# Layer 1's rest blocks: matrices in buffers of their own, names fetched three blocks ahead, the last certain block split around a turn

## The chip, the cores and the metric

The kernel runs on one core of a Trainium2 chip. The core has a matrix engine (TensorE, PE in the profile), a vector engine (DVE), a scalar engine (ACT), GpSimd (POOL) and SyncE (SP), each with a queue of its own that it works through in order, and 16 DMA engines that they all share. The metric is the device time of one execution in microseconds; less is better. Before the change the median of three runs is 1893.99 us.

## The reference, cut to what matters

The model has four layers. Each adds a graph part and a feed-forward part to `x`, of 2708 rows by 256. The change touches the feed-forward part of layer 1 only:

```python
    def _L1_ffn_ref(x, W1, b1, Wg, bg, Wd, bd):
        ...
        H = jax.nn.gelu(xf @ W1 + b1, approximate=False)
        probs = jax.nn.softmax((H @ Wg + bg) / TEMP, axis=-1)
        assign = jnp.argmax(probs, axis=-1)
        out = jnp.zeros_like(xf)
        for e in range(Wd.shape[0]):
            y = H @ Wd[e] + bd[e]
            sel = (assign == e)[:, None]
            out = out + jnp.where(sel, probs[:, e:e + 1] * y, 0.0)
        return out.reshape(orig_shape)
    ...
    x = x + _L1_ffn_ref((_layernorm(x, axis=-1))[None], L1_ffn_W1, L1_ffn_b1, L1_ffn_Wg, L1_ffn_bg, L1_ffn_Wd, L1_ffn_bd)[0]
```

There are 8 experts. A row of `H` has 1024 numbers, an expert matrix `Wd[e]` is 1024 by 256, and each row goes to one expert, the one with the largest gate value.

## The kernel before, in words

**Layer 1 in three groups of row tiles.** The 22 tiles of 128 rows (the last has 20) are worked in the groups `GROUPS1`: 8, 8 and 6 tiles. For each group the graph part streams the adjacency matrix through TensorE (L1312). Then `send1` (L1122) handles the group: it turns the normalised rows (L220), computes the hidden rows with Gelu (`hidden`, L375 and L377), computes the gate, takes the softmax and the largest value, and calls `route` (L385). `route` counts with a few small matmuls (L402 and L404) where in a list sorted by expert each row belongs. Each row's name (its number and gate value, 8 bytes) is then scattered to that place of the list `taken` in main memory (L513). `keep` (L1162) transposes the hidden rows on DVE (L1169) and writes them to `hid` in main memory; in the last group from SP (L1174 and L1177).

**Blocks.** The list is worked in blocks of 128 names of one expert. After the second group 9 blocks (`NA`) are certain to be full, whatever the third group brings; these are known while the third group's graph part still runs. The other 15 (`ALWAYS`), the rest, are laid out by `blocks` (L423) after the third group's route, because their names include that group's. More than these are worked in a branch (`run_rest`) that is taken only if some are left. So 24 blocks run in all, each with these steps in the class `Units` (L638):

- `fetch_names` (L653) gathers a block's names from `taken` with an indirect DMA of POOL (L527). It has to come after the scatters listed in `past`.
- `fetch_rows` (L663) gathers the block's 128 hidden rows, 4 KB each, from `hid` into one of four `hs` buffers with an indirect DMA of POOL (L667). It needs the block's names, and the buffer has to be free of the turn of four blocks before.
- `weights1` (L1070) loads the expert matrix (1152 KB with its bias) from SP (L1077) into one of three `wb` buffers; the load is skipped at run time if that buffer already holds this expert. Blocks are taken in the order of `in_thirds`, so that each buffer sees neighbouring blocks, often of one expert. The expert's number is read from a table in SBUF into a register of SP.
- `turn` (L673) transposes the rows on TensorE (L678, 8 instructions), and ACT copies the result to `hTs` (L679).
- The products (L729, 16 instructions of 128x256 output columns: 8 chunks of the 1024, two passes each), then the bias and the gate value on DVE (L730 and L731), and a scatter of the 128 results to `given` from POOL (L513).

`pieces` (L709) is a generator that yields after each turn and each block's products: the turn of the first block, then for every block the turn of the next and the block's own products. `send1` of the third group calls `next(fill)` to put the first pieces between its own stages. `more` (L689), called in every block, fetches names one block ahead of the rows, rows into free buffers and matrices two blocks ahead. `add` (L698) appends the rest blocks, once `blocks` has laid them out.

**What sets the order.** A scheduler puts each engine's instructions in order by dependencies and its own estimates; `after`, `engine_after` and `in_order` (L147 to L165) add orders by hand. The gate's tiles (weights of the gate, `hT`, `hrow`, the softmax and route tiles, `names`) lie in the pool `gt`, closed at L1350. SBUF that a closed pool leaves can be used by a later pool; each new tile then waits for the last readers of what lay there. When all results have landed in `given`, layer 2 reads them (`mine`, L56) and adds them to `x` (L1441).

The functions that the change touches:

Of the kernel before, what the change touches and what calls it, by code (L numbers as in the profile page):

```python
# [66 lines left out]
def adj_ffn4(ctx: ExitStack, tc: tile.TileContext, a: dict, out: bass.AP):  # L67
# [570 lines left out]
    class Units(Blocks):  # L638
# [3 lines left out]
        def __init__(self, pool, given, weights, hidden):  # L642
            Blocks.__init__(self, pool, given, weights)
            self.hidden, self.named, self.places, self.got = hidden, [], [0, 0], None

            self.names = pool.tile([P, MOST, 2], F32, name="names")
            g.memset(self.names, 1.0)
            self.hs = [pool.tile([P, HC * P], F32, name="hs", tag="hs", bufs=3) for _ in range(3)]
            for h in self.hs:
                g.memset(h, 0.0)  # L650
            self.ik, self.ok, self.outputs = "taken1", "given1", 0
# [11 lines left out]
        def fetch_rows(self):  # L663
            m, n = self.named.pop(0)
            h = self.hs[self.places[1] % len(self.hs)]
            self.places[1] += 1
            i = g.indirect_dma_start(out=h, out_offset=None, in_=self.hidden[:n, :],  # L667
                                 in_offset=bass.IndirectOffsetOnAxis(ap=m[:, 0:1].bitcast(I32), axis=0),
                                 bounds_check=n - 1, oob_is_err=False)
            self.got = i.ins.name  # L670
            self.rows.append((m, h))
# [10 lines left out]
        def begin(self, items):  # L682

            self.names_todo = list(items)
            self.todo = list(items)
            self.rows_todo = len(items)
            self.more(False)

        def more(self, weights=True):  # L689
            while self.names_todo and len(self.named) + len(self.rows) < len(self.hs) + 1:  # L690
                self.fetch_names(self.names_todo.pop(0))
            while self.rows_todo and len(self.rows) < len(self.hs):
                self.fetch_rows()
                self.rows_todo -= 1
            while weights and self.todo and len(self.ahead) < 2:
                self.fetch(self.todo.pop(0))

        def add(self, items):  # L698
            self.names_todo += items
            self.todo += items  # L700
            self.rows_todo += len(items)
            self.more()
# [6 lines left out]
        def pieces(self, pool, during=None):  # L709
# [4 lines left out]
            while self.rows:  # L714
                if len(self.rows) > 1:
                    turned.append(self.turn(pool, self.rows[1][1]))
                    yield
                w2, hT = self.ahead.pop(0), turned.pop(0)
# [8 lines left out]
                q = pools["psum"].tile([P, W], F32, name="yacc", bufs=2)[:, :D]  # L727
                for f in range(HC):
                    te.matmul(q, lhsT=hT[:, f, :], rhs=w2[:, f, :], start=(f == 0), stop=(f == HC - 1))  # L729
                v.tensor_tensor(y, q, w2[:, HC, :], ALU.add)  # L730
# [327 lines left out]
    with ExitStack() as l1:  # L1058
# [5 lines left out]
        wbs, reads = {"held": []}, []  # L1064
# [5 lines left out]
        def weights1(b, e):  # L1070

            held = wbs["held"]
            if len(held) < 3:
                held.append([wbs["pool"].tile([P, 2048 + D], F32, name="wb", bufs=3), None])
# [47 lines left out]
        def send1(tiles, ready=None, fill=None):  # L1122
# [3 lines left out]
            names = gt.tile([P, GM, 2], F32, name="names", bufs=1)[:, :G]  # L1126
# [84 lines left out]
            if ready is not None:  # L1211
                for _ in range(3):
                    next(fill)
            ix = route(gt, (sel,), G, t0 * P, rows(tiles[-1]), known)
            if ready is not None:
                in_order(start, (mybir.EngineType.PE,))
                keep(*was, nc.sync)
            for i, t in enumerate(tiles):
                r = rows(t)
                scatter(taken[1], ix[:r, i, :], names[:r, i, :], N - 1, "taken1")  # L1220

# [128 lines left out]
        gate.close()  # L1350
        past = list(scattered["taken1"])
# [5 lines left out]
        for one in wbs["held"]:  # L1357
# [755 lines left out]
```

## Time and profile before

| what | value |
|---|---|
| three runs | 1893.95, 1893.99, 1900.85 us |
| profiled execution, whole time | 1890.82 us |
| its span, first to last instruction | 1889.1 us |
| mean granted TensorE clock | 0.985 |
| first and last products of L729 start | 944.9 and 1059.4 us |
| L729, matmuls | 384, median 379 ns |
| L678, transposes | 192, median 273 ns (pipelined: eight take 0.87 us in the chain) |
| L1077, matrix loads issued from SP | 24, 1152 KB each where not skipped |
| L667, L527 gathers on POOL | median 1029 and 1002 ns of POOL's time; 4.6 and 4.3 us to landing |

The stretch of the change is thus about 920 to 1072 us of the span: the last gates, the 24 blocks, and the hand-over to layer 2. A line of the timeline reads: start, duration, engine, line, operation, output and inputs, count, and in brackets the idle time of the engine before it and what ended that. A line of the waits reads: who waited, for whom, total us, times, longest. A chain of waits lists, in order of time, what the end of the span hung on.

### The profile page before, as it was taken

Reading aid. Unit: us, or ns where it says so; the run is one execution under the profiler, and the core shown is the slowest. Engines: PE = TensorE matmul, PEld = TensorE weight load, DVE = VectorE, ACT = ScalarE, POOL = GpSimd, SP = SyncE. Lnnn points to the kernel's source line nnn. Section 1 sums busy time; section 2 is a strip of 40 time slices with the busy share of each in tenths; the row PEclk is TensorE's granted clock in tenths of the full one; section 3 lists DMA queues with packets and bytes.
Section 4 is the critical chain, followed back from the end, with each engine's and each line's share of the span. In section 5 each row is a group of like instructions: output and inputs, shape, how many; then the busy total and the mean of one; then the engine's idle time right before and its main releaser. Section 6 shows DMA issues by size and latency. Waiting matters only on the chain.

```text
span 1889.1 us, 25828 instructions
## 1 busy us (share of the span) xinstructions
PE 1816.3 (96%) x9453; PEld 1331.8 (70%) x9453; DVE 1072.4 (57%) x2451; ACT 655.3 (35%) x1472; POOL 393.3 (21%) x466
## 2 busy tenths in 40 slices
PE   8999999999999999999999699998899999999998
PEld 7888788888888888887788588887566633233344
DVE  8687872443343424444532365555345498888877
ACT  8777742222223203112322223223233542132232
POOL 0015354333321002303357400000000100011020
PEclk9999999999998999999999899999899999999999
DMA  8535658887763453644777440000101000012020
GB/s 272 156 100 165 227 193 295 320 313 295 277 265 125 141 152 103 173 119 121 209 235 250 159 65 9 1 1 1 45 1 35 17 1 23 23 26 37 23 37 18
DMA packets 93214, 237.52 MB, mean 126 GB/s; under 512 B 18288, under 2 KB 49048, under 8 KB 85017
## 3 DMA queue, kind: packets, MB, share of 16 engines
q1 hardware_dynamic: 71512, 189.18, 30.9%
q0 software_dynamic: 21568, 46.61, 9.0%
q8 instruction: 78, 1.28, 0.3%
q14 instruction: 56, 0.45, 0.1%
HBM read 218.39 MB, written 30.80 MB: 132 GB/s over the span
## 4 chain that ended last, share of the span: by engine, by line
PE 40%; DMA 4%; DVE 3%; issue 2%; ACT 1%; POOL 1%; POOLq 0%; SPq 0%; ACTq 0%; DVEq 0%
PE num L2014 10%; PE ps_acc L1548 9%; PE den L2022 6%; PE ps_tmp L375 4%; PE ps_acc L1757 3%; PE ps_tmp L267 2%; PE yacc L729 2%; DMA names<-taken,b_ix 1%; DMA hs<-hid,names 1%; DMA L_gnn_a_r<-in_L_gnn_a_r 1%; PE ps_acc L267 1%; DVE e L1985 1%; DMA mine<-given 1%; PE ps_acc L678 1%; PE ps_tmp L220 0%
## 5 line engine op out<-in xcount | busy, mean ns | idle before, releaser
L1985 DVE SCALAR_TENSOR_TENSOR e<-arena,G,mask 128x1024 f32<-128x1024 f32 (+1 forms) x252 | 275.0, 1149 | 34.1 <-PE den L2022 33.2
L2014 PE MATMUL num<-e,wh 128*64 128x512 f32 (+4 forms) x1056 | 214.0, 549 | 0.7 <-ACT L_gnn_W L1368 0.3
L1548 PE MATMUL ps_acc<-hh,e 128*128 128x257 f32 x882 | 199.2, 382 | 1.7 <-ACT o L1491 1.7
L1312 PE MATMUL acc<-sup,adrow 128*128 128x256 f32 x882 | 198.5, 382 | 1.5 <-DMA adrow<-in_adjT 1.5
L943 PE MATMUL acc<-msg,wt 128*128 128x256 f32 x882 | 197.6, 381 | 1.6 <-DVE wt L893 1.2
L1312 PEld LDWEIGHTS acc<-sup,adrow 128*128 128x128 f32 x882 | 165.1, 190 | 29.4 <-issue 5.5
L1548 PEld LDWEIGHTS ps_acc<-hh,e 128*128 128x128 f32 x882 | 163.8, 190 | 29.1 <-ACT o L1491 4.3
L943 PEld LDWEIGHTS acc<-msg,wt 128*128 128x128 f32 x882 | 165.1, 190 | 27.0 <-DVE wt L893 1.8
L591 PE MATMUL ps_acc<-xTs,wa 128*128 128x256 f32 (+1 forms) x768 | 169.3, 373 | 2.6 <-DVE xTs L581 2.6
L593 ACT ACTIVATE hTs<-ps_acc,wa 128x256 f32<-128x256 f32 (+1 forms) x192 | 88.7, 464 | 235.2 <-PE yacc L625 160.8
L625 PE MATMUL yacc<-wb,hTs 128*128 128x256 f32 x736 | 168.4, 380 | 0.0
L591 PEld LDWEIGHTS ps_acc<-xTs,wa 128*128 128x128 f32 x768 | 136.6, 190 | 28.6 <-DVE xTs L581 5.1
L2014 PEld LDWEIGHTS num<-e,wh 128*64 128x64 f32 (+1 forms) x1056 | 70.1, 136 | 122.7 <-issue 104.9
L625 PEld LDWEIGHTS yacc<-wb,hTs 128*128 128x128 f32 x736 | 137.2, 190 | 17.8 <-DVE ys L627 0.5
L1540 DVE SCALAR_TENSOR_TENSOR e<-Rb,G,mask 128x640 f32<-128x640 f32 (+2 forms) x110 | 85.0, 774 | 91.1 <-PE ps_acc L1548 90.4
L2022 PE MATMUL den<-e,wh 128*32 128x512 f32 (+4 forms) x1056 | 112.3, 546 | 0.0
L1277 DVE TENSOR_SCALAR mask<-adrow 128x1024 uint8<-128x1024 f32 (+1 forms) x66 | 41.7, 632 | 120.3 <-DMA adrow<-in_adjT 120.2
L221 ACT COPY xT<-ps_tmp 128x256 f32<-128x256 f32 x76 | 26.8, 366 | 198.9 <-PE ps_tmp L220 198.4
L729 PE MATMUL yacc<-wb,hTs 128*128 128x256 f32 x384 | 88.3, 384 | 0.8 <-DMA wb<-in_L_ffn_Wdp 0.8
L893 DVE SCALAR_TENSOR_TENSOR wt<-adrow,wt 128x640 f32<-128x640 f32 (+3 forms) x67 | 71.1, 1063 | 25.4 <-ACT wt L141 25.1
L2022 PEld LDWEIGHTS den<-e,wh 128*32 128x32 f32 (+1 forms) x1056 | 33.1, 109 | 73.6 <-issue 69.6
L513 POOL DMA_INDIRECT given<-ys,xs x46 | 65.8, 1431 | 81.1 <-DVE ys L628 67.9
(472 smaller groups left out, 2631.0 us busy)
## 6 DMA issues: line engine op xcount, KB each, us to landing
adhalf<-in_adjT SPq DMA_DIRECT2D x42, 677.0 KB
wb<-in_L_ffn_W2p SPq DMA_DIRECT2D x24, 1152.0 KB
wb<-in_L_ffn_Wdp SPq DMA_DIRECT2D x24, 1152.0 KB
wa<-in_L_ffn_W1b SPq DMA_DIRECT2D x24, 1028.0 KB
adrow<-in_adjT SPq DMA_DIRECT2D x42, 512.0 KB
adrow<-in_adjT SPq DMA_DIRECT2D x42, 320.0 KB
adrow<-in_adjT SPq DMA_DIRECT2D x21, 576.0 KB
adrow<-in_adjT SPq DMA_DIRECT2D x21, 448.0 KB
```

The lines of the kernel that those rows point to most:

```text
L375: te.matmul(p[:, :w], lhsT=w1[:, c, f * P : (f + 1) * P], rhs=xnT[:, c, c0 : c0 + w], start=(c == 0), stop=(c == DC - 1))
L591: i = te.matmul(p[:, f % 2, : m * P], lhsT=w1[:, c, f * P : (f + 1) * P], rhs=xT[:, c, : m * P], start=(c == 0), stop=(c == DC - 1))
L593: s.activation(hT[:, f, : m * P], p[:, f % 2, : m * P], AF.Gelu, bias=bias[:, f : f + 1])
L625: te.matmul(q[:, k, :], lhsT=hT[:, f, k * P : (k + 1) * P], rhs=w2[:, f, :], start=(f == 0), stop=(f == HC - 1))
L729: te.matmul(q, lhsT=hT[:, f, :], rhs=w2[:, f, :], start=(f == 0), stop=(f == HC - 1))
L943: te.matmul(p[:q, n - pair[0], :], lhsT=wt[:, k : k + q], rhs=msg[:r, j, :], start=(j == 0 and n == pair[0]), stop=(j == FULL - 1 and n == ...
L1312: te.matmul(p[:q, n - pair[0], :], lhsT=ad[:, k : k + q], rhs=sup[:, jj, :], start=(jj == 0 and n == pair[0]), stop=(jj == FULL - 1 and n ...
L1540: i = v.scalar_tensor_tensor(e[:r, :w], Rb[:r, c0 : c0 + w], G[:r, j, :], mask[:r, j, c0 : c0 + w], op0=ALU.max, op1=ALU.mult)
L1548: te.matmul(p[:, : D + 1], lhsT=e[:, k : k + q], rhs=hh[:, j, :], start=(j == 0), stop=False)
L1985: v.scalar_tensor_tensor(e[:, :w], slow[:, m % 2, k, :w], G[:, j, 2 * pair + k, :], mask[:, j, c0 : c0 + w], op0=ALU.max, op1=ALU.mult)
L2014: te.matmul(num[k * DK : (k + 1) * DK, hf, :q], lhsT=wh[some, j, 2 * pair + k, :DK], rhs=e[some, :q], start=(j == 0), stop=(j == FULL), ti ...
L2022: te.matmul(den[z * Q : (z + 1) * Q, :q], lhsT=wh[some, i, 2 * pair + k, DK : DK + 1] .to_broadcast([some.stop - some.start, Q]), rhs=e[so ...
```

## The change

- The rest blocks get matrix buffers of their own: three `wb` tiles in a new pool `w1r`, opened when the gate's pool `gt` is closed, and a list `rest` of their own in `wbs` and in `Units` (`fetch_rest`). `add` fetches three of them at once; later two are kept ahead. The first load into each of the three is not conditional.
- `names` of `send1` moves from `gt` to the pool `hw` (tile `sent`).
- Names: three blocks are fetched at the start, then one ahead among the certain blocks, and up to three ahead from the ninth row gather on.
- The third group's route is put before the products of block 1 (`range(2)` in place of `range(3)`), and the last pair's transposes on DVE are ordered behind the third DVE instruction of the route.
- The row gather of the eighth block is ordered behind the last scatter into `taken`.
- For the ninth block, the last certain one (`late`), the turn of the next block no longer stands before its products but before the last two of its eight chunks, with TensorE's order fixed.

```diff
@@ -646,6 +646,7 @@
             self.names = pool.tile([P, MOST, 2], F32, name="names")
             g.memset(self.names, 1.0)
             self.hs = [pool.tile([P, HC * P], F32, name="hs", tag="hs", bufs=3) for _ in range(3)]
+            self.past, self.border, self.rest, self.rest_ahead = None, None, [], []
             for h in self.hs:
                 g.memset(h, 0.0)
             self.ik, self.ok, self.outputs = "taken1", "given1", 0
@@ -667,6 +668,8 @@
             i = g.indirect_dma_start(out=h, out_offset=None, in_=self.hidden[:n, :],
                                  in_offset=bass.IndirectOffsetOnAxis(ap=m[:, 0:1].bitcast(I32), axis=0),
                                  bounds_check=n - 1, oob_is_err=False)
+            if self.past is not None and self.places[1] == self.border - 1:
+                after(i, self.past)
             self.got = i.ins.name
             self.rows.append((m, h))
 
@@ -682,23 +685,36 @@
         def begin(self, items):
 
             self.names_todo = list(items)
+            self.border = self.border or len(items)
             self.todo = list(items)
             self.rows_todo = len(items)
+            for _ in self.hs:
+                self.fetch_names(self.names_todo.pop(0))
             self.more(False)
 
         def more(self, weights=True):
-            while self.names_todo and len(self.named) + len(self.rows) < len(self.hs) + 1:
-                self.fetch_names(self.names_todo.pop(0))
             while self.rows_todo and len(self.rows) < len(self.hs):
+                if not self.named:
+                    self.fetch_names(self.names_todo.pop(0))
                 self.fetch_rows()
                 self.rows_todo -= 1
+            while self.names_todo and len(self.named) < (3 if self.places[1] >= self.border else 1):
+                self.fetch_names(self.names_todo.pop(0))
             while weights and self.todo and len(self.ahead) < 2:
                 self.fetch(self.todo.pop(0))
+            if weights:
+                self.fetch_rest(2)
+
+        def fetch_rest(self, most):
+            while self.rest and len(self.rest_ahead) < most:
+                self.rest_ahead.append(self.weights(self.border + self.at[1], expert_of(self.rest.pop(0))))
+                self.at[1] += 1
 
         def add(self, items):
             self.names_todo += items
-            self.todo += items
+            self.rest += items
             self.rows_todo += len(items)
+            self.fetch_rest(3)
             self.more()
 
         def run(self, pool, items):
@@ -712,10 +728,11 @@
             yield
             n = 0
             while self.rows:
-                if len(self.rows) > 1:
+                late = n == self.border - 1
+                if len(self.rows) > 1 and not late:
                     turned.append(self.turn(pool, self.rows[1][1]))
                     yield
-                w2, hT = self.ahead.pop(0), turned.pop(0)
+                w2, hT = (self.ahead or self.rest_ahead).pop(0), turned.pop(0)
                 m, _ = self.rows.pop(0)
                 self.more()
                 if during is not None:
@@ -725,8 +742,13 @@
                 y = (pool.tile([P, D], F32, name="ys", bufs=2) if self.outputs % 5 < 2 else
                      work.tile([P, D], F32, name="xn"))
                 q = pools["psum"].tile([P, W], F32, name="yacc", bufs=2)[:, :D]
+                begin = len(nc.cur_bb.bb.instructions)
                 for f in range(HC):
+                    if late and f == HC - 2 and self.rows:
+                        turned.append(self.turn(pool, self.rows[0][1]))
                     te.matmul(q, lhsT=hT[:, f, :], rhs=w2[:, f, :], start=(f == 0), stop=(f == HC - 1))
+                if late:
+                    in_order(begin, (mybir.EngineType.PE,))
                 v.tensor_tensor(y, q, w2[:, HC, :], ALU.add)
                 i = v.tensor_scalar(y, y, m[:, 1:2], None, op0=ALU.mult)
                 self.last = i.ins.name
@@ -1061,7 +1083,7 @@
         b1 = tp.tile([P, HC], F32, name="b1")
         g.dma_start(b1, a["L1_ffn_b1"])
         hw = l1.enter_context(tc.tile_pool(name="h1", side="right", reuse_waits="tile", bufs=1))
-        wbs, reads = {"held": []}, []
+        wbs, reads = {"held": [], "rest": []}, []
 
         def in_thirds(n):
 
@@ -1069,9 +1091,10 @@
 
         def weights1(b, e):
 
-            held = wbs["held"]
+            held = wbs["held" if b < NA else "rest"]
             if len(held) < 3:
-                held.append([wbs["pool"].tile([P, 2048 + D], F32, name="wb", bufs=3), None])
+                held.append([wbs["pool" if b < NA else "more"].tile(
+                    [P, 2048 + D], F32, name="wb", bufs=3), None])
             wb, was = held[b % 3]
             held[b % 3][1] = e
             i = nc.sync.dma_start(wb, a["L1_ffn_Wdp"][bass.ds(e, 1)].rearrange("e p n -> p (e n)"),
@@ -1123,7 +1146,7 @@
 
             G = len(tiles)
             t0 = tiles[0]
-            names = gt.tile([P, GM, 2], F32, name="names", bufs=1)[:, :G]
+            names = hw.tile([P, GM, 2], F32, name="sent", bufs=1)[:, :G]
             lg = gt.tile([P, G, E], F32, name="lg", tag=f"lg{G}")
             pairs = [[(i, (i - i0) * P, rows(tiles[i])) for i in range(i0, min(i0 + 2, G))]
                      for i0 in range(0, G, 2)]
@@ -1209,15 +1232,22 @@
             g.tensor_copy(names[:, :, 0:1].bitcast(I32), choice1[:, t0 : t0 + G, :])
             v.tensor_copy(names[:, :, 1:2], best)
             if ready is not None:
-                for _ in range(3):
+                for _ in range(2):
                     next(fill)
+            routed = len(nc.cur_bb.bb.instructions)
             ix = route(gt, (sel,), G, t0 * P, rows(tiles[-1]), known)
             if ready is not None:
                 in_order(start, (mybir.EngineType.PE,))
+                ranked = [k.name for k in nc.cur_bb.bb.instructions[routed:]
+                          if k.engine == mybir.EngineType.DVE][2]
+                kept = len(nc.cur_bb.bb.instructions)
                 keep(*was, nc.sync)
+                engine_after(kept, mybir.EngineType.DVE, ranked)
             for i, t in enumerate(tiles):
                 r = rows(t)
                 scatter(taken[1], ix[:r, i, :], names[:r, i, :], N - 1, "taken1")
+            if ready is not None:
+                work1.past = scattered["taken1"][-1].name
 
         psum_pool(sums, 4, 0)
         gsum = sums.enter_context(
@@ -1348,13 +1378,14 @@
         rest = blocks(hw, gt, known, MOST - NA, P, "B", done=full[2])
         too_many = count_left(hw, (rest[2], ALWAYS))
         gate.close()
+        wbs["more"] = l1.enter_context(tc.tile_pool(name="w1r", reuse_waits="tile", bufs=1))
         past = list(scattered["taken1"])
         items = [(rest, b, past, taken[1], False) for b in in_thirds(ALWAYS)]
         more = [(rest, b, past, taken[1], False) for b in range(ALWAYS, MOST - NA)]
         work1.add(items)
         for _ in between:
             pass
-        for one in wbs["held"]:
+        for one in wbs["rest"]:
             one[1] = None
         work1.run_rest(hc, more, left[0])
 
```

## The prediction

> **What bounds the kernel now.** Blocks are numbered 0 to 23 in the order in which they run: 0 to 8 are the certain ones, 9 to 23 the rest. I began with the page: who is busy, then where TensorE isn't.
>
> ```profile
> PE 1816.3 (96%) x9453; PEld 1331.8 (70%) x9453; DVE 1072.4 (57%) x2451; ACT 655.3 (35%) x1472; POOL 393.3 (21%) x466
> ...
> L729 PE MATMUL yacc<-wb,hTs 128*128 128x256 f32 x384 | 88.3, 384 | 0.8 <-DMA wb<-in_L_ffn_Wdp 0.8
> ```
>
> TensorE is busy 96% of the span, and the change takes no matmul away, so it can only win TensorE's idle time around L729 (the second products of 24 blocks). Next TensorE's waits from 925 to 1095 us:
>
> ```profile
> PE ps_tmp L1446 <- DVE x L1441: 12.2, 2, 11.7
> PE ps_acc L678 <- DMA hs<-hid,names: 6.4, 3, 4.2
> ...
> PE yacc L729 <- DMA wb<-in_L_ffn_Wdp: 0.8, 1, 0.8
> ```
>
> (Columns: total us, times, longest.) The first is the hand-over to layer 2, which the change doesn't touch. The second, three turns (L678) that waited for gathered rows, is what can be won. TensorE's timeline places them:
>
> ```profile
> 976.99 3.62 PE L729 MATMUL yacc<-wb,hTs 128*128 128x256 f32 x16
> 984.79 1.35 PE L678 MATMUL ps_acc<-ident,hs 128*128 128x128 f32 x8 [4.19 <-DMA hs<-hid,names]
> 985.94 5.06 PE L729 MATMUL yacc<-wb,hTs 128*128 128x256 f32 x16
> 990.83 1.04 PE L678 MATMUL ps_acc<-ident,hs 128*128 128x128 f32 x8
> ...
> 1005.87 1.07 PE L678 MATMUL ps_acc<-ident,hs 128*128 128x128 f32 x8 [1.68 <-DMA hs<-hid,names]
> ...
> 1010.91 1.06 PE L678 MATMUL ps_acc<-ident,hs 128*128 128x128 f32 x8 [0.52 <-DMA hs<-hid,names]
> ```
>
> The 4.19 us stand before the turn of block 9, and block 8's products, whose inputs were there, stand behind it. What block 9 waited for is in the chain of waits and on POOL's timeline:
>
> ```profile
> 973.04 3.75 DMA names<-taken,b_ix
> 976.79 2.96 issue
> 979.75 0.03 POOLq L527
> 979.78 0.19 issue
> 979.97 4.69 DMA hs<-hid,names
> 984.66 0.14 issue
> 984.79 1.35 PE ps_acc L678 x8
> ```
>
> ```profile
> 964.37 0.92 POOL L513 DMA_INDIRECT taken<-names,r_ix  x1 [0.31 <-issue]
> 965.59 1.07 POOL L667 DMA_INDIRECT hs<-hid,names  x1 [0.30 <-issue]
> 966.97 1.01 POOL L513 DMA_INDIRECT given<-xn,names  x1 [0.31 <-issue]
> 973.04 1.11 POOL L527 DMA_INDIRECT names<-taken,b_ix  x1 [5.06 <-DVE ys L730]
> ```
>
> Block 9's names can't be read before the last of six scatters into `taken`. It is issued at 964.37 and takes 7.9 us to land (the trace's figure for it), so 972.3; the name behind the arrow is only the event that came last. Then names 6.2 us to landing, rows 4.7. Last, busy time by stretch (PE, PEld, DVE, ACT, POOL, then clock, DMA share, GB/s):
>
> ```profile
> 958.00:965.00 7.00, 7.00 (x46) 6.22 (x45) 6.06 (x19) 2.15 (x4) 5.47 (x6) 1.00 0.37 82
> 965.00:981.00 16.00, 15.60 (x80) 13.51 (x79) 2.69 (x7) 3.22 (x6) 6.53 (x7) 1.00 0.96 318
> 981.00:985.00 4.00, 0.20 (x2) 0.24 (x3) 0.42 (x2) 0.00 (x0) 3.04 (x3) 1.00 0.99 356
> 985.00:990.00 5.00, 5.00 (x21) 4.28 (x20) 0.00 (x0) 1.07 (x2) 2.55 (x3) 0.66 0.61 228
> ```
>
> The DMA engines are a third busy until 965 and full from there to 985, while the latencies above are paid. After the gap the clock falls to 0.66.
>
> **What the Trainium skill says.** "TensorE: Matmul & The Clock Gate", section on the HAM clock gate: after an idle window of about 3.4 us TensorE runs at half clock until it has been busy for as long. The trace agrees: after 4.19 us idle, the turn and block 8 take 1.35 and 4.85 us in the chain against 0.87 and 3.46 elsewhere; after 1.68 us idle nothing is slower. "DMA: Bandwidth & Descriptors", section "Anatomy of one DMA": DMA engines don't wait for semaphores, the issuing sequencer does; so one waiting DMA holds everything behind it on its queue. POOL shows it (5.06 us above), and SP too: hidden rows ready at 947.5 were issued at 949.30, behind a matrix load that waited. Same page, section "Issuing engines are not separate DMA queues": all DMAs share the 16 engines. The trace agrees: `taken` scatters land in 3.2 us in the quiet stretch and in 7.9 us in the full one.
>
> **The change part by part.**
>
> *Route before block 1* (two `next(fill)`, not three). The route's matmuls move from 952.82 to behind the second turn, which ends at 949.36: they end some 3.4 us earlier less any wait for their input. That input (`r_m`) was ready at 950.05; the two 0.7 us transposes that `ranked` now holds back cost its chain about 0.5 us, so it comes at 949.5: TensorE may idle 0.1 to 0.7 us, I take 0.2. Block 1 follows 1.46 us later, and the row indices come near 952.5 instead of 955.82. The held-back transposes (1.9 us on DVE, beside TensorE) make the last hidden rows 1 to 2 us later; only rest blocks read those, over 15 us on.
>
> *Scatters before the rows of block 7* (`past`). POOL issues them at 1.3 us each from about 953.7 rather than 957.86; the last at 960.2 rather than 964.37. The rows of block 7 go from 956.52 to about 962.8. Half their turn stood in TensorE's order at 964.5 (the 20 transposes at 962.99), though it is only due at 972.2: if the order stays, TensorE waits 1 to 3 us; if it follows the rows, nothing. I take 0.3.
>
> *Matrices of the rest in their own buffers.* An issue on SP that lasts 0.33 us moves 1.18 MB, one of 0.07 to 0.10 is skipped (same expert). Real loads stand at 963.89, 969.42, 972.87 (blocks 6 to 8), 976.76, 981.09, 991.49 (9 to 11), 995.82, 1000.14, 1004.68 (12 to 14). The change adds no load but moves 9 to 11 forward, to when their expert number is known (957.5 before, about 955 now) and the gate's tiles are read for the last time (hidden rows landing near 957, the block table near 958 to 961). 3.5 MB at some 400 GB/s (the trace's 356 to 426 GB/s when full) are 8.8 us, so 958 to 967, much of it in the stretch that was a third busy. Load 6, issued at about 964 on the same queue, lands by 970, due at 972. No load is then left between 976 and 989.
>
> *Names three ahead.* The names of 9, 10 and 11 go out in a row once the scatters have landed: 960.2 plus 7 us, estimated between the 5.2 of a scatter before and the 7.9 of the last, is 967. POOL reaches them at about 968; plus 6.2 is 974.3, rows plus 4.7 to 8.2 (range of row gathers) 979 to 982.5. In steady state a row gather no longer waits for names just requested (1.9 and 0.8 us of POOL waits at 988 and 1032). The moved `names` tile and the three names at the start cost nothing: POOL is idle for 20 us behind them, up to 943.
>
> *Block 8 split.* Six eighths of block 8 (0.75 x 3.46 = 2.6 us) now run before the turn of block 9, which is due at 980.6 + 2.6 = 983.2 plus the 0.2 above. Rows landed by 982.5 leave no gap. Won: 4.19 idle, and (1.35 + 4.85) - (0.87 + 3.46) = 1.87 of slow clock, together 6.06.
>
> *The waits at 1005.87 and 1010.91* (1.68 + 0.52). The rows of block 13 were issued at 997.55, behind POOL's backlog from its waits around 970, and took 8.2 us. POOL needs about 4 us per block against TensorE's 4.33, so it recovers slowly. Now the backlog starts some 5 us earlier and loads 9 to 11 are out of the way; I place that gather at 986 to 990, landing by 998, when it is due. Won 2.2; 0.3 kept as residue.
>
> Next late is the load of block 22 (0.84 us at 1051.8), unchanged. The hand-over to layer 2 hangs on the last scatter into `given`, issued just behind block 23, and moves along whole.
>
> Sum: 6.06 + 2.2 - 0.2 - 0.3 - 0.3 = 7.5 us. The profiled execution spans 1889.1 us and takes 1890.8 in all; it becomes 1883.3. The median shown is 1893.99, 3.2 us above it; the same difference gives 1886.5.
>
> **The rivals.**
>
> *Half of it* (latencies bind). Loads moved to 958 to 967 lie on top of the scatters, names and rows of blocks 7 and 8. For it: latency doubles on a full DMA; slack at 983.2 is 1 to 4 us. Against: the bytes are the same and spread wider. If the rows of 9 land at 985 (1.6 us late, too short to slow the clock), the later waits stay and block 7's turn costs 1 us: 7.5 - 1.6 - 1.9 - 0.7 = 3.3 us, 1890.7.
>
> *More.* Residues vanish and the 0.84 goes: 6.06 + 2.2 + 0.84 = 9.1 us, 1884.9; with a measurement low by 0.1%, 1883.
>
> *Slower: SP's queue blocked.* Row indices still lie in the gate pool. If one rest buffer overlaps them, or another late reader, its load stands at SP's head until the scatters have landed (967 to 970), with load 6 behind it. Then three loads (8.8 us) and load 6 (2.9) land at 979 to 982, block 6 (due 972) starts 7 to 10 us late and pays 1.9 for the clock: 9 to 12 lost against 8.3 won. It decides from a release at about 966, and each us later costs one: at 970 it is 3.7 slower, 1897.7. For it: SP did block so at 949. Against: the matrices need 27.6 KB per partition, and the gate's large tiles (`wg`, `xT4`, `hT`, `lT`, `hrow`), made first, sum to about 26 KB.
>
> **How the numbers follow.** Forecast 0.55, half 0.22, more 0.10, slower 0.13. A measurement of this kernel can't tell less than about 0.5% (9.5 us) from no change. The forecast and the half lie inside it but for the forecast's upper end with noise; "more" is on its edge. Faster than 1884.5: half of "more" and a quarter of the forecast, 0.19, with 0.01 for the unforeseen. Slower than 1903.5: a third of the slower case and a little for a second such block, 0.06. The range reaches from 1881.5 (9 us and noise of 3) to 1894.5 (the half failing whole).
>
> **What would show it.** The last `taken` scatter near 960; three rest loads before that of block 6; no idle before the turn of block 9, clock 1.0 throughout; no wait near 1000. Wrong if TensorE idles before block 6 or 7, if the first names of the rest still go out after 971, or if the gain exceeds 9.5 us.

## The result and the profile after

The changed kernel takes 1907.7 us (median of 9 runs, 1903.93 to 1912.73), the kernel before on the same chip 1898.47 (1893.95 to 1902.49): ratio 1.006, 95% interval 1.0045 to 1.0075, so slower beyond noise: 9.2 us between the medians, about 11 us by the ratio. The prediction had 1886.5 us, in a range of 1881.5 to 1894.5. The profiled execution of the changed kernel is the longest of its nine (1912.73 us, span 1911.0) and is 21.9 us longer in span than that of before. I cut both at the first turn (L678, now L681) and at the end of block 23's products (L729, now L749):

| us | before | after | difference |
|---|---|---|---|
| start to first turn | 941.68 | 949.20 | 7.5 |
| the 24 blocks ("the stretch") | 118.12 | 129.15 | 11.0 |
| behind the blocks | 829.30 | 832.65 | 3.4 |

The first row is run-to-run: two more profiles of the changed order of instructions start their turns at 941.64 and 948.95, two of the kernel before at 947.61 and 957.57. The other two rows are the change: three profiles of the changed order have 125.6 to 129.2 us in the second row and 832.2 to 833.8 in the third, three of the kernel before 118.1 to 122.5 and 827.2 to 829.3.

TensorE's waits from 925 to 1095 us (total, times, longest):

```profile
PE ps_acc L681 <- DMA hs<-hid,names: 15.6, 4, 11.2
PE ps_tmp L1477 <- DVE x L1472: 12.1, 2, 10.5
...
PE yacc L749 <- DMA wb<-in_L_ffn_Wdp: 0.2, 1, 0.2
```

The matrices come in time, but the wait for gathered rows, which was to vanish, grew from 6.4 to 15.6 us. TensorE's timeline shows where:

```profile
976.36 3.62 PE L749 MATMUL yacc<-wb,hTs 128*128 128x256 f32 x16
991.16 1.94 PE L681 MATMUL ps_acc<-ident,hs 128*128 128x128 f32 x8 [11.18 <-DMA hs<-hid,names]
992.89 5.27 PE L749 MATMUL yacc<-wb,hTs 128*128 128x256 f32 x16
998.00 1.04 PE L681 MATMUL ps_acc<-ident,hs 128*128 128x128 f32 x8
998.87 6.21 PE L749 MATMUL yacc<-wb,hTs 128*128 128x256 f32 x28
1004.92 1.04 PE L681 MATMUL ps_acc<-ident,hs 128*128 128x128 f32 x8
...
1020.28 1.94 PE L681 MATMUL ps_acc<-ident,hs 128*128 128x128 f32 x8 [2.97 <-DMA hs<-hid,names]
```

The x28 is block 7 with six eighths of block 8: the split is there, and block 9's turn (1004.92) waits for nothing. But the wait has moved two blocks forward, to block 7's turn, and is longer. POOL's timeline says why:

```profile
961.43 1.04 POOL L668 DMA_INDIRECT hs<-hid,names  x1 [1.82 <-issue]
962.78 2.11 POOL L513 DMA_INDIRECT taken<-sent,r_ix  x1 [0.31 <-DVE xn L752]
...
970.37 0.92 POOL L513 DMA_INDIRECT taken<-sent,r_ix  x1 [0.30 <-DMA taken<-sent,r_ix]
971.59 1.06 POOL L527 DMA_INDIRECT names<-taken,b_ix  x1 [0.30 <-issue]
972.96 1.01 POOL L513 DMA_INDIRECT given<-xn,names  x1 [0.30 <-issue]
981.86 1.05 POOL L668 DMA_INDIRECT hs<-hid,names  x1 [7.89 <-issue]
983.21 1.00 POOL L513 DMA_INDIRECT given<-xn,names  x1 [0.31 <-issue]
984.52 1.05 POOL L527 DMA_INDIRECT names<-taken,b_ix  x1 [0.30 <-issue]
993.46 1.02 POOL L668 DMA_INDIRECT hs<-hid,names  x1 [7.88 <-PE ps_acc L681]
```

The name issued at 971.59 is that of block **7**, behind all six scatters; in the kernel before the names of 7 and 8 stood ahead of them. Its rows go out 10.3 us later (981.86) and release the turn 9.3 us after that (991.16). Block 8's name comes only at 984.52. POOL, in order, stands in both pauses. The names of blocks 9 to 11 follow at 994.79 to 997.41, where the prediction had about 968 (7.5 us go off for the later start: 987). Busy time by stretch (columns as in the prediction):

```profile
950.00:958.00 8.00, 7.74 (x66) 6.77 (x64) 4.06 (x19) 4.90 (x9) 3.79 (x4) 1.00 0.34 76
...
964.00:981.00 17.00, 15.75 (x84) 13.41 (x82) 6.44 (x22) 3.22 (x6) 7.83 (x8) 1.00 0.97 252
981.00:991.00 10.00, 0.00 (x0) 0.00 (x0) 0.00 (x0) 0.00 (x0) 3.10 (x3) 0.58 0.97 404
991.00:998.00 7.00, 6.84 (x25) 5.93 (x26) 0.00 (x0) 1.17 (x2) 3.63 (x4) 0.63 0.28 85
```

TensorE, DVE and ACT stand still for 10 us while the DMA engines are full; then TensorE runs at 0.63 clock and the DMA engines are a quarter busy. Six matrices make up most of that traffic: SP issues the three of the rest at 964.1, 966.8 and 967.7, those of blocks 6 to 8 at 973.1, 976.6 and 980.5.

Behind the blocks the chain of waits shows the other row of the table (first the kernel before, then the changed one; both start where `mine`, layer 2's read of the outputs, is issued):

```profile
1067.21 3.57 DMA mine<-given
1070.78 0.02 issue
1070.81 0.70 DVE x L1441
1071.51 0.02 issue
1071.53 3.86 DMA mine<-given
```

```profile
1085.27 2.81 DMA mine<-given
1088.08 0.02 issue
1088.10 0.70 DVE x L1472
1088.81 0.02 issue
1088.82 6.90 DMA mine<-given
```

The second read takes 6.90 us, not 3.86. What lies beside it is on POOL's timeline, before and after:

```profile
1040.24 0.80 POOL L127 DMA_DIRECT2D L_ffn_Wr<-in_L_ffn_Wr  x1
...
1050.49 0.73 POOL L1407 DMA_DIRECT2D w_l<-in_L_gnn_WT  x1 [4.28 <-DMA hs<-hid,names]
```

```profile
1085.40 0.75 POOL L127 DMA_DIRECT2D L_ffn_Wr<-in_L_ffn_Wr  x1 [4.94 <-DMA given<-xn,names]
...
1088.89 0.74 POOL L1438 DMA_DIRECT2D w_l<-in_L_gnn_WT  x1
```

Layer 2's small weights (seven loads) went out from 20 us ahead of the end of the last product on; now they go out with `mine`. Their tiles lie in the closed gate pool's room, which was free before and now belongs to the rest's matrices until the last block; series 5 below tests this.

### The profile page after: what moved, and what is told of

The parts are those of the page before. It is cut to its first block, busy times and chain, and to the rows that moved or that the text cites. A ratio compares the mean times of both kernels' runs of the same rounds, so it can differ in the third digit from the quotient of the medians.

```text
span 1911.0 us, 25825 instructions
## 1 busy us (share of the span) xinstructions
PE 1821.4 (95%) x9453; PEld 1333.1 (70%) x9453; DVE 1072.4 (56%) x2451; ACT 655.8 (34%) x1472; POOL 393.0 (21%) x466
## 5 line engine op out<-in xcount | busy, mean ns | idle before, releaser
L749 PE MATMUL yacc<-wb,hTs 128*128 128x256 f32 x384 | 89.3, 387 | 0.2 <-DMA wb<-in_L_ffn_Wdp 0.2
```

## The experiments

There were five series, each on one chip with runs of the kernel before beside it (1906.64, 1893.14, 1909.65, 1892.14 and 1911.0 us). In every profile of the first, third and fifth, and in none of the others, some copies of the turns on ACT (and some additions of the bias on DVE) start late, ended by "remote", which stands for no releaser that the profile names. The kernel before has it too (a profile in series 3). It covers row waits, so the fourth series decides on sizes. "Tail" is the time behind the blocks.

**Names one more ahead** (changed kernel, series 1, again in 3 and 4):

```diff
-... len(self.named) < (3 if self.places[1] >= self.border else 1):
+... len(self.named) < (3 if self.places[1] >= self.border else 2):
```

> The changed kernel, but names kept two blocks ahead of the row gathers among the certain blocks instead of one, so that the names of blocks 7 and 8 are fetched before the scatters into taken. The measure is the block stretch, from the start of the first turn to the end of the last second product: 118.1 us in the kernel before, 129.2 us in the changed one. Theory 'names' (the rule of one name ahead made names and rows of blocks 7 and 8 a chain of four DMAs one after another): the wait before block 7 shrinks from 11.2 to at most 2 us and the stretch to 114-119 us, so about 1893-1898 us. Rival 'loads' (the three matrix loads moved forward fill the DMA engines and stretch every scatter, name and row gather to 9-10 us): the wait only moves to block 9, whose names still have to follow the scatters that land 9.9 us after issue; a wait of 6 us or more there, stretch 124-130 us.

**The rest's loads later**: not ahead of the certain blocks' last load (series 1).

```diff
 def add(self, items):
-    self.fetch_rest(3)
 def more(self, weights=True):
-    if weights:
+    if weights and not self.todo:
         self.fetch_rest(2)
```

> The changed kernel with its names rule, but the rest's matrices are not fetched when the rest is laid out; they follow in SP's order behind the last certain block's matrix, into their own buffers. Theory 'loads': latencies fall back to 4-6 us, the wait before block 7 shrinks to at most 3 us, block stretch 115-119 us. Rival 'names': the serial chain names 7, rows 7, names 8, rows 8 stays; names of block 7 at the same place behind the scatters, wait before blocks 7 and 8 together 6 us or more, stretch 122-128 us.

**The names rule alone**, put into the kernel before, and **both mended**:

> The kernel before with the changed names rule alone (three at the start, then one fetched behind the row gather, three ahead from block 9 on). Theory 'names': the name of block 8 now stands behind the scatters on POOL, so its rows come late: a new wait of 3-6 us before block 8, and the old wait before block 9 is not shorter; stretch 120-126 us. Rival 'loads': the names rule costs nothing by itself; stretch 116-119 us.

> The changed kernel with both: names two ahead among the certain blocks, and the rest's matrices behind the last certain block's. Both theories expect the best of the four: no wait over 1 us before blocks 7 and 8, at most 3 us before block 9, stretch 109-115 us, so 3-9 us faster than the kernel before. If a wait over 4 us is left before block 9, then scatters, names and rows in a row are late without any extra load on the DMA engines, and a third cause is needed.

Measured: names two ahead 1.002 (1.001 to 1.0031), stretch 121.19 us, no wait for rows; loads late 1.0094 (1.0063 to 1.0124), stretch 135.72, rows waits 4.59 and 5.93 us at blocks 7 and 8; names rule alone 1.0013 (1.0003 to 1.0023), stretch 124.78, its waits put down to ACT; both mended 1.0011 (0.9994 to 1.0027), stretch 117.96. So the row waits go with the names. Loads late alone brought no gain that can be seen: its two row waits still make 10.5 us, against 15.6 us for all four in the changed kernel's profile, and its ratio (four runs) lies above the 1.0055 to 1.0079 that the changed kernel has in other series; in this one it was not run. Its stretch is longer than either theory had. The sizes are blurred by ACT: both mended was expected 3 to 9 us faster than before and isn't, and how much the names rule costs by itself stays open here.

**Series 2**: the kernel before against itself, the changed kernel without `past`, and parts of the change in the kernel before: the split of block 8 (with `late = n == 8`), then split and route (`range(2)` and `engine_after`).

> The kernel before, unchanged, as a control and for its profile beside the others on the same chip. Ratio 1.000 within 0.2%. Theory 'names' and 'loads' both: block stretch 117-120 us as in the first profile. A third theory, 'ScalarE held up' (on the last chip the copies of turned rows, L682, began 2 to 3 us after their input was there, while the DMA engines were full, and that is what the mended kernels lost): if the kernel before shows the same waits on this chip, the stretch is 120-126 us and they are the chip's, not the change's.

```diff
-if ready is not None:
-    work1.past = scattered["taken1"][-1].name
```

> The changed kernel without the rule that puts the rows of block 7 behind the last scatter into taken. The order in which every engine's instructions stand is the same with and without it, so every theory expects the changed kernel again: 0.4-0.8% slower than before, 8 us or more of idle TensorE before block 7, block stretch 127-132 us. It is also a second profile of the changed kernel's order.

> The kernel before, with block 8 split around the turn of block 9 and nothing else. By the prediction's working 2.6 us of products run ahead of that turn: the wait before block 9 falls from 4.2 to at most 1.6 us and the slow clock behind it goes, 4.5 us in all; stretch 113-115 us, 0.2% faster. If DMA latency varies by some us from chip to chip, the gain is anything from 0 to 6 us.

> The kernel before with the split of block 8 and the route put before block 1 (with the transposes held back), but its own names rule and its own matrix loads. By the prediction's working the scatters go out some 4 us earlier, so the wait before block 9 goes whole: 6 us less than before from that alone, 7 to 8 with the later waits; stretch 110-112 us, 0.3-0.4% faster. If instead the loads that the change moved were needed for the gain, it stays at the 4.5 us of the split.

Before itself 1.0009 (0.9999 to 1.0018), stretch 119.67. Without `past` the instructions of TensorE, DVE, ACT and POOL come in the same order as in the changed kernel, so that rule does nothing, and this is the change measured again: 1.0055 (1.0038 to 1.0072), stretch 127.94, tail 833.81, and the wait again before block 7:

```profile
989.15 1.94 PE L681 MATMUL ps_acc<-ident,hs 128*128 128x128 f32 x8 [8.92 <-DMA hs<-hid,names]
```

Split alone: 1.0008 (0.9997 to 1.002), stretch 121.07. The wait before block 9, expected to be at most 1.6 us, is 4.75, and 0.65 and 2.72 us stand later. The kernel before had 4.19 in its first profile and 7.56 in this series, so one profile of each can't show the 2.6 us of work moved ahead. First the kernel before, then the split:

```profile
994.09 1.94 PE L678 MATMUL ps_acc<-ident,hs 128*128 128x128 f32 x8 [7.56 <-DMA hs<-hid,names]
```

```profile
987.69 1.94 PE L678 MATMUL ps_acc<-ident,hs 128*128 128x128 f32 x8 [4.75 <-DMA hs<-hid,names]
...
1001.14 1.06 PE L678 MATMUL ps_acc<-ident,hs 128*128 128x128 f32 x8 [0.65 <-DMA hs<-hid,names]
...
1008.39 1.08 PE L678 MATMUL ps_acc<-ident,hs 128*128 128x128 f32 x8 [2.72 <-DMA hs<-hid,names]
```

Split and route: 0.9999 (0.9986 to 1.0011), stretch 118.9. POOL's timeline:

```profile
964.77 0.92 POOL L513 DMA_INDIRECT taken<-names,r_ix  x1 [0.30 <-issue]
...
971.33 1.02 POOL L527 DMA_INDIRECT names<-taken,b_ix  x1 [0.31 <-issue]
...
980.36 1.00 POOL L667 DMA_INDIRECT hs<-hid,names  x1 [6.69 <-PE ps_acc L678]
```

Its first turn is at 944.95, so the last scatter (964.77) comes 19.8 us behind it, where the kernel before had 22.7. But block 9's rows go out 9.0 us after their name and its turn (990.19) comes 9.8 us after them, against 6.9 and 4.8 in the kernel before: 3.57 us of wait stay, and 1.06, 1.98 and 0.91 us later. The earlier start went into slower transfers.

**Series 3**: before itself, names two ahead again, both mended again, and the kernel before **without the rest's matrix loads** (this one leaves them out and multiplies by old matrices).

> The kernel before, unchanged, as a control and for its profile on the same chip as the next three. Ratio 1.000 within 0.2%; block stretch 117-122 us. If ScalarE's copies of turned rows (L682 or L679) start 2 us or more after their input is there in this profile too, those delays belong to the chip; if only in the others, to the kernels.

> The kernel with names two ahead (e1) once more, on another chip. There its TensorE lost 6.5 us to ScalarE copies that began late for no reason the profile names. Theory 'names' as it stands now: without those the stretch is 113-117 us and the kernel 0.1-0.3% faster than before. Rival 'full DMA engines': the early loads only move the shortage, block 9's rows come late or blocks 11 to 14 wait instead, stretch 118-122 us, ratio 1.000-1.003.

> The kernel with names two ahead and the rest's matrices behind the last certain block's (e6) once more, on another chip. Against e9 it tells what the early loads are worth once the names are in time. 'Full DMA engines': loads in the quiet stretch before 967 are worth something, so this one is slower than e9 by 2-4 us; 'early loads in the way': it is faster than e9 by 2-4 us; if within 1 us of it, the place of these loads doesn't matter.

```diff
 def weights1(b, e):
+    if b >= NA:
+        return wb.rearrange("p (f d) -> p f d", d=D)
     i = nc.sync.dma_start(wb, ...)
```

> The kernel before with the matrix loads of all rest blocks (9 to 23) left out: they multiply by the matrices that the certain blocks left in the buffers. That takes 9 real loads of 1.18 MB off the DMA engines, two of them before the wait of block 9. Theory 'full DMA engines' (from 965 to 1012 us of the first profile the engines are some 95% busy, and what is won in latency in one place is lost in another): the wait before block 9 falls to 3 us or less, the later waits go, stretch 109-113 us. Rival 'chain' (scatter, names, rows one after another are late by themselves): the wait before block 9 stays 4 us or more with its slow clock, stretch 115-118 us.

Ratios 1.0 (0.9989 to 1.0011), 1.0023 (1.001 to 1.0037), 1.0 (0.9986 to 1.0014), 0.9995 (0.9982 to 1.0008); stretches 122.48, 122.09, 117.87 and 120.46 us. ACT's timeline of the kernel before, then TensorE's:

```profile
990.27 1.07 ACT L679 COPY hTs<-ps_acc 128x512 f32<-128x512 f32 x2 [13.43 <-remote]
```

```profile
990.91 1.97 PE L678 MATMUL ps_acc<-ident,hs 128*128 128x128 f32 x8 [10.03 <-ACT hTs L679]
```

The 13.43 us are all of ACT's idle time before this copy; the turn that it copies was done by 980.9, so it starts about 10 us late, and TensorE waits for it. This is why the loads' own weight couldn't be read from the run without them here (the engines are 0.91 busy from 965 to 1012 us of the first profile, a little less than its expectation says).

**Series 4**, the deciding one: the changed kernel again, then names two ahead, both mended, and before without the rest's loads.

> The changed kernel, unchanged, beside the next two on one chip. Theory 'names': 0.4-0.8% slower than the kernel before wherever it runs, and slower than e13 by 0.4% or more. If it is within 0.2% of e13, the names rule isn't what made it slow and the whole account falls.

> The change with names two ahead (as e1 and e9). Theory 'names': no wait for rows of over 2 us before blocks 7 and 8, 0.4% or more faster than e12; against the kernel before 0.9975-1.003, at the lower end on a chip without ScalarE's late starts. Rival 'loads': wait before block 7 or 9 of 5 us or more, within 0.3% of e12.

> The change with names two ahead and the rest's matrices behind the last certain block's (as e6 and e11). Both earlier pairs had it 0.1-0.2% faster than with early loads; if that holds again, the early loads cost 2-4 us even with the names in time. 'Full DMA engines' in its first form (loads in the quiet stretch are worth something) expects the opposite, 0.1-0.2% slower than e13.

> The kernel before with the matrix loads of blocks 9 to 23 left out (the rest multiplies by the certain blocks' last matrices), once more. 'Full DMA engines': on a chip without late starts of ScalarE the wait before block 9 falls to 3 us or less and the ratio to 0.995-0.997; with them, no wait for rows over 1 us as in e10, ratio near 0.999. 'Chain': the wait before block 9 stays 4 us or more.

| series 4 | ratio (95%) | stretch | tail |
|---|---|---|---|
| changed | 1.0079 (1.0058 to 1.01) | 125.55 | 832.21 |
| names two ahead | 1.0041 (1.0026 to 1.0057) | 118.66 | 831.40 |
| and loads late | 1.0008 (0.9998 to 1.0018) | 115.59 | 831.15 |
| before, no rest loads | 0.9974 (0.9964 to 0.9984) | 114.11 | 826.56 |

The names are worth 0.0038 x 1892 = 7.2 us (four and seven runs, whose intervals just miss each other; the stretch has 6.9 us less). The two runs have the same order of instructions on TensorE, DVE and ACT, and differ on POOL's queue alone, in 14 places. TensorE's timeline, changed kernel, then names two ahead:

```profile
982.30 1.94 PE L681 MATMUL ps_acc<-ident,hs 128*128 128x128 f32 x8 [10.33 <-DMA hs<-hid,names]
```

```profile
979.00 1.94 PE L681 MATMUL ps_acc<-ident,hs 128*128 128x128 f32 x8 [2.84 <-DMA hs<-hid,names]
985.46 1.07 PE L681 MATMUL ps_acc<-ident,hs 128*128 128x128 f32 x8 [0.50 <-DMA hs<-hid,names]
...
1007.82 1.07 PE L681 MATMUL ps_acc<-ident,hs 128*128 128x128 f32 x8 [2.93 <-DMA hs<-hid,names]
```

Both come out a little under what was expected: 0.38% for 0.4, and a wait of 2.84 us stays before block 7 where at most 2 were allowed. The early loads are worth another 6.2 us (these intervals don't overlap either); here all four engines have the same order, only SP's loads stand elsewhere. In the profiles the stretch falls by less, 3.1 us; in the pairs of series 1 and 3 by 3.2 and 4.2 us, with ratios 0.0009 and 0.0023 apart. So 3 to 6 us. With names two ahead, block 8's rows were issued at 970.88 and released its turn at 985.46, 14.6 us later; the stretch line shows full DMA engines:

```profile
970.88 1.05 POOL L668 DMA_INDIRECT hs<-hid,names  x1 [0.30 <-issue]
```

```profile
964.00:982.00 18.00, 15.16 (x76) 13.13 (x75) 3.29 (x11) 3.96 (x8) 9.14 (x10) 0.91 1.01 363
```

With the loads late the DMA engines are half empty from 964 to 982, and blocks 7 and 8 wait for nothing: block 8's rows, issued at 974.29, are there when its turn comes at 983.75, within 9.5 us. But the engines fill behind 982, and the wait is back at block 9:

```profile
964.00:982.00 18.00, 18.00 (x100) 15.98 (x99) 6.71 (x22) 4.30 (x8) 11.93 (x12) 1.00 0.54 186
982.00:1000.00 18.00, 13.73 (x68) 11.49 (x67) 2.38 (x6) 2.81 (x6) 12.16 (x12) 0.91 0.98 386
```

```profile
994.05 1.84 PE L681 MATMUL ps_acc<-ident,hs 128*128 128x128 f32 x8 [3.23 <-DMA hs<-hid,names]
```

Without the rest's loads block 9's rows land within 4.3 us (issued 981.89, turn 986.21) and the later waits are gone, but 4.36 us before block 9 stay, where the theory of full DMA engines allowed at most 3 (and a ratio of at most 0.997):

```profile
986.21 1.94 PE L678 MATMUL ps_acc<-ident,hs 128*128 128x128 f32 x8 [4.36 <-DMA hs<-hid,names]
```

That much is the chain of scatters, name and rows even on freer engines (0.76 busy from 964 to 982, against 0.93 in the first profile of the kernel before).

**Series 5**: the tail. All ten profiles with the rest's own room so far have tails of 830.7 to 833.8 us, all eight without it 826.6 to 829.3. I made layer 2's small loads late in the kernel before, and took the room away from the changed kernel with both faults mended.

```diff
 work1.run_rest(hc, more, left[0])
+work1.very_end = scattered["given1"][-1].name
...
-tc.add_manual_dep(i, work1.at_end, ...
+tc.add_manual_dep(i, work1.very_end, ...
```

> The kernel before with one thing moved: layer 2's seven small loads on POOL's queue (L127, L121, L1401, L1403, L1408) stand behind the last scatter into given instead of some 20 us ahead of it, as they do in every kernel with the rest's own room. The profiles so far differ after the blocks: from the last second product to the end of the span 826.6 to 829.3 us without that room, 830.7 to 833.8 us with it. Theory: the small loads collide there with layer 2's reads of the outputs (mine), and that is the whole difference: this run has 831 to 833 us after the blocks and a ratio of 1.0015 to 1.003. Rival: the difference comes from the stretch itself (DMA work left over, another order on PE or DVE): 827 to 829 us and a ratio of 1.000.

```diff
-held = wbs["held" if b < NA else "rest"]
+held = wbs["held"]
-wbs["more"] = l1.enter_context(tc.tile_pool(name="w1r", ...
```

> The changed kernel with names one more ahead and the rest's loads after the last certain one (as in the run with 1.0008), and now with the rest's matrices back in the three old buffers; the split of block 8, the moved route and three names in a row stay. Theory: layer 2's small loads go out early again, 827 to 829 us after the blocks, and with a stretch of 115 to 119 us the ratio is 0.998 to 0.9995. Rival, that the room is not what delays the small loads: 831 to 833 us after the blocks and a ratio near 1.001. Second rival, that the old buffers hold the loads back: the stretch grows to 121 us or more with waits for wb.

Small loads late: 1.0013 (1.0002 to 1.0024), tail 831.99. Old room: small loads early again, tail 827.21. The second read of `mine` in the one and in the other:

```profile
1092.37 6.29 DMA mine<-given
```

```profile
1099.80 3.81 DMA mine<-given
```

So the room delays the small loads, and their delay alone makes the tail longer, by about 4 us in the profiles (2.7 to 5.4, by which of the eight it is set against). The total grew by 2.5 us (0.4 to 4.6). The ratio of the second is 1.0033 (1.0023 to 1.0043), its stretch 131.14: the second rival came true as well, the old buffers hold the late loads back:

```profile
1009.19 12.59 PE L748 MATMUL yacc<-wb,hTs 128*128 128x256 f32 x44 [12.23 <-DMA wb<-in_L_ffn_Wdp]
```

No version that uses the right matrices is measurably faster than the kernel before; the one without the rest's loads is (0.9974), but it leaves work out.

## Why the prediction was wrong, by its steps

- *Names of blocks 7 and 8*: this step failed most. The prediction priced the names of the start and of blocks 9 to 11, let the rows of block 7 go "from 956.52 to about 962.8", and put what the new rule does to the names in between at nothing. The three names at the start did cost nothing, as it says (POOL is idle for 20.22 us behind them). But the new order in `more` fetches a name only behind a row gather and keeps one, so the names of 7 and 8 fell behind the scatters: block 7's rows went at 974.3 in the time of before (981.86 less 7.5), and TensorE waited 11.18, 8.92 and 10.33 us before block 7 in three profiles; 7.2 us in series 4. The prediction's 0.3 us for block 7 was that term. Two of its own signs of being wrong came true here: idle time before block 7, and first names of the rest after 971.
- *Matrices of the rest*: time and place were right. Taking 7.5 us off for the later start, the loads begin at 956.6 (964.11 in its own time), and no load waits over 2.8 us at the head of SP's queue there, so the slower rival's mechanism fell. The failed term is the room on the DMA engines: they are full from 964 to 991 in its own time, scatters that were taken to land in 5.2 to 7.9 us took 8.7 to 10.1, a name 9.5 for 6.2 (block 7's), rows 9.3 to their turn for 4.7 to 8.2 (block 7's too). The "half" rival named that reason, but put it at 1.6 us for block 9 and 1 us for block 7; with the names mended it is 6.2 us in series 4. The Trainium skill, "DMA: Bandwidth & Descriptors", section "Issuing engines are not separate DMA queues", says that DMAs run on the same 16 engines and interleave, whichever engine issued them. The trace agrees: with the same order on POOL, block 8's rows took 14.6 us beside SP's early loads and at most 9.5 us with those late.
- *Hand-over "moves along whole"*: failed, by about 4 us in the profiles. The prediction asked what the new room would wait for, and not who had used it next.
- *Route*: moved as said, with no idle. The six scatters start 2.6 us earlier, not 4.2, and end at 962.9 in the time of before, not 960.2. Here too the names are in the way: in the changed kernel POOL waits 3.05 us for block 5's name, and with the old rule or with names two ahead the scatters start 4.0 us earlier.
- *Block 8 split and the later waits* (6.06 + 2.2 us): in the changed kernel no idle stood before block 9, but that was luck: TensorE was held up at block 7 so long that block 9's rows were there. With names and loads mended 3.23 us stand there again. As time, the gain is small: the stretch is then 115.6 us against 118.1 and 119.7 in two profiles of before in other series without ACT's delay, 2.5 to 4 us, and the tail gives it back: 1.0008. The later waits stayed (1.04 and 0.52 us there).
- *Clock*: right in the main; 0.58 to 0.63 in and behind the 11 us pause. The 3.4 us that the prediction goes by are no sharp limit here: turns behind waits of 2.84 us (names two ahead, series 4) and 2.97 us (the changed kernel) took 1.94 us, one behind 2.93 us (the first of these runs) 1.07 us.

In series 4 the changed kernel is 14.9 us slower than before (1.0079): 7.2 for the names, 6.2 for the loads, and 1.5 that stay with both mended. This adds up by construction, since each part is a step from one run to the next. The 1.5 us are the loss behind the blocks (about 4 in the profiles, 2.5 as a total in series 5) less what split, route and three names bring; that these bring 2.5 to 4 us is read from single profiles, and no run shows it as time. The parts also depend on their order: the loads' 6.2 us hold with the names in time.

Open: why ACT's copies start late in three series; what the names rule costs alone without that; and a version with names two ahead, late loads and a room of its own that leaves layer 2's small tiles free, which was not tried.

## What to carry to other kernels

When a prefetch rule is rewritten, write out the whole order of the in-order queue before and after, and look at every request that changes sides of a slow one; here each index had to be fetched a step further ahead than the rows it serves. Before a bulk load is moved "into a quiet stretch", look for chains of small dependent transfers in that stretch: here they paid for it. A pool put into freed room also needs the question which later tile was allocated there, and how early it was filled.

## What the runs showed of the hardware

Small transfers become slow on full DMA engines. In the kernel before, the first of the six scatters into `taken` landed in 3.2 us (engines 0.37 busy) and the last in 7.9 us. In the changed kernel the four issued from 966.50 to 970.37 took 8.7 to 10.1 us (0.97 busy); the gather of block 6's names, issued at 957.27, took 3.4 us, that of block 7's, at 971.59, took 9.5.

Copies on ACT started up to about 10 us late, and biases on DVE late too, for a reason outside the profile, in every profile of three series and in none of the two others. The kernel before took 1906.6 to 1911.0 us in those three, against 1892.1 to 1893.1 in the two. It isn't a fixed property of a chip, as far as the record goes: series 1, with the late copies, and series 2, without, have the same chip number. Nor is the stretch most of it: of the 12 to 18 us by which the span of the kernel before was longer in series 3 than in its two other profiles, 10 to 16 lie ahead of the first turn.
